# Layer 1's side products on a Trainium2 core: paired convolution taps, a bank sum on VectorE, and B with C in one step

## The chip, the cores and the metric

The kernel runs on one core of a Trainium2 chip. The metric is the device time of one launch in microseconds (us); lower is better. Engines are named as in the profile: PE is TensorE (matmul), PEld its weight loads, DVE is VectorE, ACT is ScalarE, POOL is GpSimd, and SP issues the DMAs. Everything is computed in fp32.

## The reference, cut to what matters

Four layers follow one another on x of shape (4, 64, 64, 64). Layers 0, 2 and 3 are not touched by the change. Layer 1 runs a state-space scan ("mamba") twice on each image, once along rows (w) and once along columns (h). For every one of 64 sequences of 64 tokens, with 192 channels and 96 states per channel:

```python
x1, res = jnp.split(x @ in_w.T, 2, axis=-1)
xc = causal depthwise convolution of x1 with K = 4 taps + conv_b      # cut
x1 = jax.nn.silu(xc)
A = -jnp.exp(jnp.clip(A_log, -5.0, 5.0))
x_dbl = x1 @ xproj_w.T
delta = jax.nn.softplus(x_dbl[..., :DTR] @ dproj_w.T + dproj_b)
B = x_dbl[..., DTR:DTR + N];  C = x_dbl[..., DTR + N:]
# selective_scan(u=x1): for each state n
c = jnp.exp(jnp.minimum(reversed cumulative sum of delta * A, 15.0))  # cut
x = jnp.cumsum(delta * u * B * c, axis=1) / (c + 1e-06)
y = jnp.einsum('bldn,bln->bld', x, C) + u * D
return y * jax.nn.silu(res) @ out_w.T
```

## The kernel before, in words

`layer1` calls `scan1` twice for each of the four images (d = 0 for w, d = 1 for h), so there are eight scans. A scan handles 4,096 tokens as 16 chunks of 256 tokens. A chunk has 2 tiles of 128 tokens; a tile's 128 partitions are two sequences of 64 tokens. Each tile goes through its 96 states in 12 blocks of 8 states, and each block in two units. A chunk is therefore 48 units, a scan 768 units, all scans 6,144 units. This text counts the units of a chunk from 0 to 47; units 0 and 24 open its tiles.

**The main work of a unit k** is the same everywhere:

- `expand(k+4)`: eight PE products write `z`; ACT makes two sigmoids of it, `e` and `r` (L1007). In every second unit POOL builds the two matrices `tB` and `dC` (L1015) and in the others SP copies a part of `r` across partitions by two DMAs (L1021).
- `weigh(k+1)` on DVE multiplies `e` by the token weights (L1030).
- `scan(k)` on PE computes the cumulative sums into the PSUM tile `S`, of which there is only one.
- `divide(k-1)` on DVE multiplies `S` into `r` (L1053). The next `scan` may not write `S` before that.
- `collect(k-1)` on PE adds the unit's share of y into the PSUM tile `y`, also a single one, of two banks. After the 24th unit of a tile ACT copies both banks into the SBUF tile `yt` (L1073).

**The side work** of a chunk is cut into steps: `pre` makes what the next chunk needs, `post` finishes a tile. A step is a small group of products on PE into the spare 128 columns of a `z` tile, an eviction on DVE one unit later, and sometimes elementwise work (`fs`) on DVE or ACT. `aside(k)` hands out one step per unit. The steps of `pre` are, in order: `conv` twice (8 products each), `res` twice, `dt` twice, `bc` four times (tile 0 and 1, B and C each), two steps of elementwise work alone, `after` twice, `utok` twice. `post` has `turn` (it transposes y and adds its two banks with it), a gate, and `out`. In a chunk they fall into units 1 to 18, and one more `turn` into unit 26. The gates multiply by a sigmoid (`res_gate`, and `yg` at L948); the four operations called `soft` (L885 to L888) make the softplus.

**The order** is written out by hand: `in_order` chains the instructions of PE, DVE, ACT and POOL, each engine on its own, in the order in which the loop issues them. In unit k DVE does `divide(k-1)`, then the eviction of the previous unit's step, then `weigh(k+1)`, then `fs`. PE does `scan(k)`, the `z` of k+4, `collect(k-1)`, then the step's products. ACT does the two sigmoids, then, where a tile has ended, the copy of y. SP is not chained. Chunk 0 of each scan has its side steps done one after another by `now`, before the loop.

Of the kernel before, what the change touches and what calls it, by code (L numbers as in the profile page):

```python
# [54 lines left out]
class Net:  # L55
# [229 lines left out]
    def setup_l1(self, sp, pp, d):  # L285
# [6 lines left out]
        P = slice(0, C) if d == "w" else slice(C, 2 * C)  # L292
        self.mm(ps[P, 0 : 2 * D1], hd, inw)
        w["wres"] = self.ctile([2 * C, D1], f"{n}_wres")[P]
        nc.vector.tensor_copy(w["wres"], ps[P, D1 : 2 * D1])
        cw = sp.tile([2 * C, 4, D1], F32, name=f"{n}_cw", tag="cw")[P]
        nc.sync.dma_start(cw, self.a[f"{n}_cw"].unsqueeze(0).to_broadcast([C, 4, D1]))
        w["wk"] = self.ctile([2 * C, 4, D1], f"{n}_wk")[P]
        for k in range(4):
            nc.vector.tensor_tensor(w["wk"][:, k, :], ps[P, 0:D1], cw[:, k, :], ALU.mult)  # L300
# [425 lines left out]
    def scan1(self, b, d, p, x1, x2):  # L726
# [30 lines left out]

        def pre(q, cx):
            n = f"b{b}{d}_{q}"
            T = lambda shape, tag, **k: p["q"].tile(shape, F32, name=f"{n}_{tag}", tag=tag, **k)  # L760
# [6 lines left out]
            dl = T([128, NTL, D1 + 16], "dl")  # L767
            d0 = s2 = dl[:, :, 0:D1]
# [8 lines left out]
            def conv(h):  # L777
                def mm(ps):
                    for i in range(2):
                        for k in range(4):  # L780
                            self.mm(
                                ps[0:DH, i, :], w["wk"][:, k, h * DH : (h + 1) * DH],
                                tokens(q, k)[:, 2 * i : 2 * i + 2], k == 0, k == 3,
                            )
# [8 lines left out]
            def res(h):  # L793
                def mm(ps):
                    for i in range(2):
                        self.mm(
                            ps[0:DH, i, :], w["wres"][:, h * DH : (h + 1) * DH],
                            tokens(q, 3)[:, 2 * i : 2 * i + 2],
                        )
# [19 lines left out]
            def bc(i, x):  # L819

                def mm(ps):
                    for s in range(2):
                        t0 = i * 128 + s * 64
                        for h in range(2):
                            self.mm(
                                ps[64 * s : 64 * s + 64, x, 0:N1], us[:, h, t0 : t0 + 64],
                                w["xbc"][:, h, x, s : s + N1].rearrange("p (i t) -> p t i", t=2),
                                h == 0, h == 1,
                            )

                def ev(ps):
                    nc.vector.tensor_copy(
                        BC[:, i, 2 * x : 2 * x + 2].rearrange("p t n -> p (t n)"), ps[:, x, 0:N1]
                    )
                    for s in range(2 * x):
# [6 lines left out]
            def utok(i):  # L842
# [6 lines left out]
                def ev(ps):  # L849
                    nc.vector.tensor_tensor(  # L850
                        half(wt[:, i]), half(dl[:, i, 0:D1]), ps[:, :, 0:DH], ALU.mult
                    )
# [3 lines left out]
            def after(i):  # L856

                def mm(ps):
                    for x in range(2):
                        for j in range(2):  # L860
                            c = (2 * x + j) * GC
                            self.mm(
                                ps[64 * j : 64 * j + 64, x, :], dl[:, i, c : c + 64], self.tri_after
                            )
# [12 lines left out]
            def first():  # L877
                nc.gpsimd.memset(dl[:, :, D1:], 0.0)
                nc.scalar.activation(u, dv, AF.Abs)
                nc.scalar.activation(u, u, AF.Sigmoid, bias=self.ln_half, scale=-1.0)  # L880
                nc.scalar.activation(s2, u, AF.Square)
# [3 lines left out]
                lambda: STT(po, po, ATANH[2], s2, ALU.add, ALU.mult),  # L885
                lambda: STT(po, po, ATANH[1], s2, ALU.add, ALU.mult),
                lambda: STT(po, po, ATANH[0], u, ALU.add, ALU.mult),
                lambda: STT(d0, dv, 0.0, po, ALU.max, ALU.add),  # L888
# [8 lines left out]
            step(bc(0, 0), first)  # L897
            step(bc(0, 1), res_gate[1])
            step(bc(1, 0), soft[0])
# [403 lines left out]
```

## Time and profile before

| what | us |
|---|---|
| median of 3 runs | 19620.61 |
| the runs | 19591.22 to 19622.32 |
| the profiled execution, its own time | 19619.08 |
| its span, first to last instruction | 19617.3 |
| the eight scans of layer 1 (sum of eight stretches of the trace) | 15222.6 |
| PE, DVE, ACT, POOL busy in the span | 17894.3, 16196.6, 12514.8, 8675.7 |
| mean granted PE clock | 0.965 |

The eight stretches are as long as the others within 1.1%, and in them the granted clock is 0.99 to 1.00. The change touches only these stretches (and a few instructions of the setup). A unit of the loop can be recognised in the trace by its `divide`, so the time from one `divide` to the next is the length of a unit. A matmul of the source is two matmul instructions in the trace, except a transpose, which is one.

### The profile page before, as it was taken

The numbers are of one execution on the slowest core, as the hardware profiler recorded it, in microseconds if no ns is written. First come the engines' busy times: TensorE is split into PE (matmuls) and PEld (weight loads), VectorE is DVE, ScalarE is ACT, GpSimd is POOL, SyncE is SP. The second block draws the span as 40 slices with busy tenths as digits, with TensorE's granted clock in tenths as the row PEclk, the third lists the DMA queues.
The fourth block names the chain that finished last, engine by engine and source line by source line (L and its number), as shares of the span: only waits on it lengthen the run. The fifth ranks groups of instructions, "written<-read, shape, count | busy, mean of one in ns | idle before, by whom it ended". The sixth has DMA issues, their size and how long they took to land. (4 is left out here: it accounts for less than half of the span.)

```text
span 19617.3 us, 623762 instructions
## 1 busy us (share of the span) xinstructions
PE 17894.3 (91%) x271560; PEld 11600.9 (59%) x271560; DVE 16196.6 (83%) x18938; ACT 12514.8 (64%) x15787; POOL 8675.7 (44%) x7068
## 2 busy tenths in 40 slices
PE   7999999997799999999779999999977999999996
PEld 2666666662266666666226666666622666666662
DVE  7788878887878887888788888888788888788878
ACT  4677767774467766776446776777644677677764
POOL 0455545551045554555115555555511555455551
PEclk9999999998999999999899999999988999999998
DMA  0233333330033333333003333333300333333320
GB/s 7 69 83 82 84 73 81 82 83 5 1 74 82 82 81 75 83 82 79 4 1 79 82 82 77 81 81 81 76 4 3 81 81 82 76 82 82 82 72 2
DMA packets 559944, 1265.03 MB, mean 64 GB/s; under 512 B 160568, under 2 KB 161824, under 8 KB 557216
## 3 DMA queue, kind: packets, MB, share of 16 engines
q1 hardware_dynamic: 557216, 1225.12, 26.0%
q8 instruction: 2144, 35.13, 0.8%
q14 instruction: 584, 4.78, 0.1%
HBM read 6.24 MB, written 4.19 MB: 1 GB/s over the span
## 5 line engine op out<-in xcount | busy, mean ns | idle before, releaser
L1007 ACT ACTIVATE b_k_e<-b_z,shift 128x768 f32<-128x768 f32 x6144 | 5533.4, 901 | 4501.7 <-PE b_z L120 3747.1
L1015 POOL TENSOR_TENSOR b_k_tB<-b_BC,tri 128x512 f32<-128x512 f32 x3072 | 3440.0, 1120 | 7456.0 <-PE b_u_S L120 6691.9
L1053 DVE TENSOR_TENSOR b_k_r<-b_u_S,b_k_r 128x768 f32<-128x768 f32 x6144 | 5858.1, 953 | 998.7 <-DMA b_k_r<-b_k_r 302.4
L1030 DVE TENSOR_TENSOR b_k_e<-b_k_e,b_wt 128x768 f32<-128x768 f32 x6144 | 6171.8, 1005 | 29.5 <-ACT b_k_e L1007 29.5
L120 PE MATMUL b_u_S<-b_k_e,b_k_tB 64*64 64x192 f32 x98304 | 5429.1, 335 | 598.5 <-DVE b_k_r L1053 507.2
L1007 ACT ACTIVATE b_k_r<-b_z,ln_eps 128x768 f32<-128x768 f32 x6144 | 5490.3, 894 | 0.0
L120 PE MATMUL b_y<-b_k_r,b_k_dC 64*64 64x192 f32 x98304 | 5194.2, 323 | 64.8 <-ACT b_yt L1073 62.4
L120 PE MATMUL b_z<-A,b_T 48*64 48x384 f32 x49152 | 5219.2, 487 | 4.5 <-ACT b_k_r L1007 4.3
L120 PEld LDWEIGHTS b_y<-b_k_r,b_k_dC 64*64 64x64 f32 x98304 | 3918.4, 133 | 2173.1 <-issue 1490.7
L1015 POOL TENSOR_TENSOR b_k_dC<-b_BC,ident 128x512 f32<-128x512 f32 x3072 | 4756.3, 1548 | 2.8 <-DMA b_BC<-b_BC 2.4
L120 PEld LDWEIGHTS b_u_S<-b_k_e,b_k_tB 64*64 64x64 f32 x98304 | 3280.0, 133 | 1867.4 <-DVE b_k_r L1053 1030.3
L120 PEld LDWEIGHTS b_z<-A,b_T 48*64 48x64 f32 x49152 | 1915.2, 135 | 225.3 <-DVE b_yg L922 57.8
L120 PE MATMUL d_y<-d_o,ident 128*128 128x512 f32 x1024 | 656.8, 775 | 416.5 <-DVE d_o L435 416.2
L432 POOL COPY l_state<-d_h 128x2 f32<-128x2 f32 x256 | 119.8, 468 | 1633.7 <-DVE d_h L429 1633.7
L120 PE MATMUL a_y<-a_o,ident 128*128 128x512 f32 x1024 | 575.9, 690 | 225.2 <-DVE a_o L435 223.3
L432 POOL COPY l_state<-a_h 128x2 f32<-128x2 f32 x256 | 110.5, 432 | 1418.9 <-DVE a_h L429 1418.9
L120 PEld LDWEIGHTS d_y<-d_o,ident 128*128 128x128 f32 x1024 | 213.6, 231 | 816.1 <-DVE d_o L435 620.3
L429 DVE TENSOR_TENSOR_SCAN a_h<-a_a,l_state,a_g 128x512 f32<-128x512 f32 x512 | 629.4, 1270 | 29.4 <-DVE a_g L418 0.5
L429 DVE TENSOR_TENSOR_SCAN d_h<-d_a,l_state,d_g 128x512 f32<-128x512 f32 x512 | 628.9, 1269 | 25.5
L407 ACT ACTIVATE d_a<-d_dl,l_A 128x512 f32<-128x512 f32 x512 | 339.2, 711 | 355.2 <-DVE d_dl L521 183.2
L407 ACT ACTIVATE a_a<-a_dl,l_A 128x512 f32<-128x512 f32 x512 | 336.1, 710 | 319.5 <-DVE a_h L429 160.9
L120 PEld LDWEIGHTS a_y<-a_o,ident 128*128 128x128 f32 x1024 | 189.9, 205 | 590.8 <-DVE a_o L435 377.3
(359 smaller groups left out, 11829.5 us busy)
## 6 DMA issues: line engine op xcount, KB each, us to landing
b_k_r<-b_k_r SPq DMA_DIRECT2D x6144, 192.0 KB, 2.9
b_BC<-b_BC SPq DMA_DIRECT2D x512, 12.0 KB, 1.8
xin<-in_x SPq DMA_DIRECT2D x16, 256.0 KB, 5.8
out<-d_so SPq DMA_DIRECT2D x32, 128.0 KB, 2.3
l1w_cw<-in_l1w_cw SPq DMA_DIRECT2D x1, 192.0 KB, 3.4
l1h_cw<-in_l1h_cw SPq DMA_DIRECT2D x1, 192.0 KB
t_l1w_in<-in_l1w_in SPq DMA_DIRECT2D x1, 144.0 KB, 2.2
t_l1w_xbc<-in_l1w_xbc SPq DMA_DIRECT2D x1, 144.0 KB
```

The source lines that it names most:

```text
L120: self.nc.tensor.matmul(out, lhsT=lhsT, rhs=rhs, start=start, stop=stop)
L407: nc.scalar.activation(a[:, t, :], dl, AF.Exp, scale=m["A"][:, j : j + 1])
L429: nc.vector.tensor_tensor_scan(h[:, t, :], now[:, t, :], g[:, t, :], st, ALU.mult, ALU.add)
L432: nc.gpsimd.tensor_copy(m["state"][:, 2 * i : 2 * i + 2], h[:, :, TOK - 1])
L1007: nc.scalar.activation(o.rearrange("p x (j c) -> p j x c", j=2), zin, AF.Sigmoid, bias=bias, scale=scale)
L1015: nc.gpsimd.tensor_tensor(out, m.unsqueeze(3).to_broadcast(shape), x.unsqueeze(1).unsqueeze(2).to_broadcast(shape), ALU.mult,)
L1030: nc.vector.tensor_tensor(e, e, chunks[q]["w"][:, i, :].unsqueeze(1).unsqueeze(2).to_broadcast([128, 2, 2, D1]), ALU.mult,)
L1053: nc.vector.tensor_tensor(r, S[k][:, :, 0:UC], r, ALU.mult)
```

## The change

1. **Two taps as one product.** Before, the convolution read the tokens from `x1` with 64 rows and 4 shifts: four products per output piece. Now `taps(q)` copies a chunk's tokens by two DMAs into a tile `xs` of 128 rows, the second half shifted by one token. The weights are laid out to match, and two products of 128 rows do the work of four of 64. `res` uses `xs` as well and takes the lower rows for one half and the upper rows for the other.
2. **Gates side by side.** `dl` gets a layout of four groups of 64 columns (48 used), so that `after` makes two products of 128 columns where it made four of 64. Elementwise operations on it read groups of 48.
3. **y's banks added and transposed.** ACT copies only the first bank of y to `yt`; a new DVE operation adds the second bank; `turn` then is two transposes in place of four accumulating products.
4. **B and C of a tile in one step.** `bc(i)` makes both for all 128 tokens, four products of 97 columns in place of eight of 96 that each covered 64 tokens; two DVE copies of 64 partitions each pick the even or odd order. The four `bc` steps become two, and the first two `soft` operations get steps of their own, as the last two had.

```diff
+        def taps(q):
+            xs = p["q"].tile([2 * C, QS, W + 3], F32, name=f"b{b}{d}_{q}_xs", tag="xs")
+            i, to = (3 + q * QS) * (W + 3), xs.rearrange("c h w -> c (h w)")
+            x = x1[d * C : (d + 1) * C].rearrange("c h w -> c (h w)")
+            size = QS * (W + 3)
+            nc.sync.dma_start(to[0:C], x[:, i : i + size])
+            nc.sync.dma_start(to[C:, 0 : size - 1], x[:, i + 1 : i + size])
+            return xs
...
         def pre(q, cx):
+            xs = cx["xs"]
+            if q + 1 < NQ:
+                chunks[q + 1]["xs"] = taps(q + 1)
...
-            dl = T([128, NTL, D1 + 16], "dl")
-            d0 = s2 = dl[:, :, 0:D1]
+            dl = T([128, NTL, 4, 64], "dl")
+            grouped = lambda x: x.rearrange("p i (g c) -> p (i g) c", c=GC)
+            d0 = s2 = dl.rearrange("p i g c -> p (i g) c")[:, :, 0:GC]
...
-                        for k in range(4):
+                        for k in range(2):
                             self.mm(
                                 ps[0:DH, i, :], w["wk"][:, k, h * DH : (h + 1) * DH],
-                                tokens(q, k)[:, 2 * i : 2 * i + 2], k == 0, k == 3,
+                                xs[:, 2 * i : 2 * i + 2, 2 * k : 2 * k + W], k == 0, k == 1,
                             )
...
-                    for s in range(2):
-                        t0 = i * 128 + s * 64
+                    for x in range(2):
                         for h in range(2):
                             self.mm(
-                                ps[64 * s : 64 * s + 64, x, 0:N1], us[:, h, t0 : t0 + 64],
-                                w["xbc"][:, h, x, s : s + N1].rearrange("p (i t) -> p t i", t=2),
-                                h == 0, h == 1,
+                                ps[:, x, 0 : N1 + 1], us[:, h, i * 128 : (i + 1) * 128],
+                                w["xbc"][:, h, x], h == 0, h == 1,
                             )
                 def ev(ps):
-                    nc.vector.tensor_copy(
-                        BC[:, i, 2 * x : 2 * x + 2].rearrange("p t n -> p (t n)"), ps[:, x, 0:N1]
-                    )
-                    for s in range(2 * x):
+                    for s in range(2):
+                        P = slice(64 * s, 64 * s + 64)
+                        nc.vector.tensor_copy(
+                            BC[P, i, 0:4].rearrange("p (x t) i -> p x t i", x=2),
+                            ps[P, :, s : s + N1].rearrange("p x (i t) -> p x t i", t=2),
+                        )
+                    for s in range(2):
                         nc.sync.dma_start(
...
-                        for j in range(2):
-                            c = (2 * x + j) * GC
-                            self.mm(
-                                ps[64 * j : 64 * j + 64, x, :], dl[:, i, c : c + 64], self.tri_after
-                            )
+                        self.mm(
+                            ps[:, x, :], dl[:, i, 2 * x : 2 * x + 2].rearrange("p g c -> p (g c)"),
+                            self.tri_after,
+                        )
...
-            step(bc(0, 0), first)
-            step(bc(0, 1), res_gate[1])
-            step(bc(1, 0), soft[0])
-            step(bc(1, 1), soft[1])
-            for f in soft[2:]:
+            step(bc(0), first)
+            step(bc(1), res_gate[1])
+            for f in soft:
                 step(None, f)
...
-                    for k in range(2):
-                        self.mm(
-                            ps[0:DH, h, :], yt[:, k, h * DH : (h + 1) * DH], self.ident, k == 0, k == 1
-                        )
+                    nc.tensor.transpose(ps[0:DH, h, :], yt[:, h * DH : (h + 1) * DH], self.ident)
...
-                yt = p["q"].tile([128, 2, D1], F32, name=f"{n}_yt", tag="yt", bufs=1)
-                nc.scalar.copy(yt, ys.pop(t)[:, :, 0:D1])
+                yt = p["q"].tile([128, D1], F32, name=f"{n}_yt", tag="yt", bufs=1)
+                y = ys.pop(t)
+                nc.scalar.copy(yt, y[:, 0, 0:D1])
+                sums.append(lambda: nc.vector.tensor_tensor(yt, y[:, 1, 0:D1], yt, ALU.add))
...
             if taken:
                 taken[0](taken[1])
                 taken = None
+            while sums:
+                sums.popleft()()
             S.pop(k - 1, None)
             scan(k)
```

## The prediction

> **What bounds the kernel now.** I read the page first, then the busy time of each engine in the eight stretches of layer 1, then single units in the timeline, since the shares are averages over two kinds of unit.
>
> ```profile
> PE 17894.3 (91%) x271560; PEld 11600.9 (59%) x271560; DVE 16196.6 (83%) x18938; ACT 12514.8 (64%) x15787; POOL 8675.7 (44%) x7068
> 5447.00:7350.00 1903.00, 1820.30 (x32572) 1307.69 (x32572) 1602.75 (x1926) 1342.06 (x1646) 1000.02 (x776) 1.00 0.34 82
> ```
>
> The second line is one scan: 1903 us, PE busy 1820, DVE 1603. PE looks like the bound, but its records overlap. The timeline at the start of the second tile of a chunk (unit 24 on) shows more:
>
> ```profile
> 5867.89 0.96 DVE L1053 TENSOR_TENSOR b_k_r<-b_u_S,b_k_r 128x768 f32<-128x768 f32 x1
> 5868.76 0.95 DVE L1030 TENSOR_TENSOR b_k_e<-b_k_e,b_wt 128x768 f32<-128x768 f32 x1
> 5869.85 0.96 DVE L1053 TENSOR_TENSOR b_k_r<-b_u_S,b_k_r 128x768 f32<-128x768 f32 x1
> 5870.12 0.48 ACT L1073 COPY b_yt<-b_y 128x384 f32<-128x384 f32 x1
> 5870.75 0.88 PE L120 MATMUL b_y<-b_k_r,b_k_dC 64*64 64x192 f32 x16 [0.32 <-ACT b_yt L1073]
> 5871.42 0.86 PE L120 MATMUL b_u_S<-b_k_e,b_k_tB 64*64 64x192 f32 x16
> 5872.39 0.96 DVE L1053 TENSOR_TENSOR b_k_r<-b_u_S,b_k_r 128x768 f32<-128x768 f32 x1 [0.58 <-PE b_u_S L120]
> 5873.51 1.11 PE L120 MATMUL b_z<-ident,b_yt 128*96 128x128 f32 x8
> 5874.66 0.60 DVE L922 SCALAR_TENSOR_TENSOR b_yg<-b_us,t_l1w_D,b_z 96x128 f32<-96x128 f32 x2 [1.31 <-PE b_z L120]
> 5876.05 0.95 DVE L1053 TENSOR_TENSOR b_k_r<-b_u_S,b_k_r 128x768 f32<-128x768 f32 x1
> ```
>
> A unit without side work lasts 1.96 us from divide to divide (5867.89 to 5869.85; 2.10 where POOL works beside it, 2.03 on average). DVE fills it (0.87 + 0.87 from start to start, so some 0.2 of rest), PE fills it too (0.69 + 0.66 + 0.68). And there is the loop scan, divide, scan through the single S: 0.88 + 0.96 plus about 0.1 of handover. All three ends are within 0.1 us. In a unit with side work PE adds the step's products at its end; DVE can evict them only then, and eviction, weigh and divide follow one another. So a side unit is bound by PE when its products are long, and by the chain "end of the products, eviction, weigh, fs, divide" when they are short or DVE has much to do. The start of a chunk:
>
> ```profile
> 5807.29 0.48 DVE L787 TENSOR_SCALAR b_v<-b_z,t_l1w_cb 96x256 f32<-96x256 f32 x1 [2.78 <-PE b_z L120]
> 5808.55 0.95 DVE L1053 TENSOR_TENSOR b_k_r<-b_u_S,b_k_r 128x768 f32<-128x768 f32 x1
> 5811.39 1.43 POOL L1015 TENSOR_TENSOR b_k_tB<-b_BC,tri 128x512 f32<-128x512 f32 x1 [5.68 <-PE b_u_S L120]
> 5811.83 1.53 DVE L948 TENSOR_TENSOR b_yg<-b_yg,b_us 96x512 f32<-96x512 f32 x1
> 5812.56 1.99 PE L120 MATMUL b_z<-x,l1w_wk 64*96 64x128 f32 x16
> ```
>
> DVE sat idle 2.78 us for the end of a conv: that unit is PE's. The gate at L948 took 1.53 us where the same shape takes 0.68 at L873, because POOL held something it needs.
>
> **The change, part by part.** Steps are priced from start to start of what follows, in the chunk that opens at 5801.59.
>
> *PE prices.* Conv is 16 instructions in 1.91 us (5812.56 to 5814.47), 0.120 each. The new conv is 8 instructions of 128 rows by 96 columns, 128 moving: the shape of turn, whose 8 took 1.04 (5873.51 to 5874.55, where the next scan starts), 0.130 each. [...] The row says 1.04; I take the row. New turn: two transposes; the nearest row is utok, also two transposes, 0.31 us for two at 96 columns; I take 0.34 (bounds 0.28 and 0.5). `after`: 4 full instructions for 8 half-wide ones that took 0.59; res, also 4, takes 0.61: no change. `res` may overlap its halves, 0.3 to 0.61, and does not matter: DVE with a gate ends its units. `bc` is where counting misleads:
>
> ```profile
> L120 PE MATMUL b_z<-l1w_xbc,b_us 96*64 96x96 f32 x1920 | 139.6, 263 | 0.0
> L120 PE MATMUL b_z<-l1w_wx,b_us 96*128 96x96 f32 x960 | 135.8, 285 | 0.0
> 5831.75 0.58 PE L120 MATMUL b_z<-l1w_xbc,b_us 96*64 96x96 f32 x8
> 5832.46 0.26 DVE L832 COPY b_BC<-b_z 128x96 f32<-128x96 f32 x1 [0.62 <-PE b_z L120]
> 5836.11 0.54 DVE L885 SCALAR_TENSOR_TENSOR b_dp<-b_dp,b_dl 128x384 f32<-128x384 f32 x1
> 5836.27 1.29 POOL L1015 TENSOR_TENSOR b_k_tB<-b_BC,tri 128x512 f32<-128x512 f32 x1 [3.40 <-PE b_u_S L120]
> ```
>
> The first two lines are groups (count, busy us), the others the timeline. The old products 64 columns wide go in pairs beside each other: 139.6 us for 1920 against 135.8 for 960 full-wide ones. The new step has wx's shape, 8 instructions, 1.07 us; two old steps took 2 x 0.51. So PE gains nothing, and what was spread over four units stands in two.
>
> *DVE prices.* The bank sum, 128x192 from PSUM and SBUF, is L850's shape: 0.35. The new copy on ACT is half as wide as 0.48; I take 0.30. A `bc` eviction is two copies of 192 elements: between 0.25 for 96 (L832) and 0.42 for 256 (L866), so 0.35, starting 0.26 apart. That the PSUM read has a step of two is in no row: 0.30 to 0.55, and I take 0.35.
>
> **Stage A, units 0 to 4** (t = 0 at 5801.59). Before: copy of y 2.24, first collect of the new tile 2.86, conv 3.67 to 5.66, divide(2) 6.96, divide(3) 11.70, divide(5) 17.4. After: DVE comes free at 0.87 but the sum waits for the copy, which ACT does behind both sigmoids: 2.54. Sum 2.62 to 2.97; weigh starts 2.89 in place of 0.87; divide(1) 3.8 in place of 1.96. The collect waits for the sum: 3.11; conv 3.87 to 4.98, hiding the late DVE; eviction 5.02, weigh 5.42, divide(2) 6.28. Turn 7.02 to 7.43 in place of 7.70 to 8.81; skip, weigh 7.99, and the gate behind POOL's tB as before, divide(3) 10.3. The second conv is then ready (10.6) before divide(3) ends (11.3), so only a part of its saving shows: divide(5) 15.85. Gain 1.55, of 2 x 0.87 + 0.70 = 2.44 that PE saves.
>
> **Stage C, units 24 to 27** (t = 0 at 5867.89), the same without a conv as cover. Sum 2.60 to 2.95; weigh 2.87; divide(25) 3.74 in place of 1.96; scan(26) can only start at 4.75 in place of 3.53: a loss of 1.2. Turn gives 0.70 back: divide(27) 8.68 in place of 8.16. Loss 0.5.
>
> **Stage B, units 9 to 12** (t = 0 at divide(9), 5830.89; before, divide(13) at 11.24). The first bc ends at 2.00 in place of 1.44; copies 2.06 and 2.32, weigh 2.58, gate 3.44, divide(10) 4.04 (before 3.32). Second bc 4.13 to 5.27; copies 5.33 and 5.59; weigh 5.85 to 6.8. Now POOL's tB, released by a scan that ends at 6.08, waits for weigh and is first in line; soft0 wants to start at 6.72 and stands behind it until 7.8. [...] The trace agrees twice (L948 1.53 against 0.68; L888 1.39 beside a POOL operation), but at soft0 before it shows 0.54, because tB came 0.16 after it (the lines above). [...] Then divide(12) 10.4 and divide(13) 12.6: loss 1.35. Before, soft0 and soft1 ran under bc products; now their units have only DVE work, 0.87 + 0.87 + 0.46 = 2.2.
>
> **Other parts.** The two taps DMAs of a chunk stand in SP's queue before the DMAs of r, 1.1 us of issue, and wait for nothing recent; an r has over 4 us from issue to use and lands in 2.9: nothing. If that cover were gone, every chunk would wait up to 1 us. POOL's memset is unchanged. In chunk 0 of a scan the slow conv (3.7 and 2.0 us there) is halved, bc and the sum give part back, and the first taps DMA lies beside the 5 us in which DVE builds A3: 0 to 4 us gain, I take 2. Sum: 128 x (-1.55 + 0.5 + 1.35) = +38, minus 8 x 2 = +22 us. The profiled execution took 19619 and the median is 19621, so this gives 19640.
>
> **The rivals.**
> 1. [...] If soft0 gets in front of tB in stage B, 0.9 us per chunk comes back at once, some 0.6 net of what runs behind: with the base loss gone, 128 x (-0.3) - 16 = -54; with cheaper evictions (0.30) as well another 0.2 per chunk: 19540 to 19565. For it: before, soft0 was first. Against: tB hangs on the scan's end, 0.5 us before soft0.
> 2. *Evictions with a step of two (slower).* Each 0.1 us on the four copies of a chunk lengthens the chain twice by 0.2 (the z products wait for these copies too): 128 x 0.4 = 51. At 0.55, a half rate, 19640 + 102 = 19742; with a longer sum 19770. It decides from 0.38 on, where the sum passes +0.2%. Against: L866 shows a PSUM copy at 1 ns an element.
> 3. *PE was the bound everywhere.* Then 2.44 + 0.70 per chunk are saved, 128 x 3.1 = 400, 19220. Against: the stall chain of stage C.
> 4. *Conv does not halve*, because 128-row products with alternating taps cost more than turn: at 0.24 each stage A loses its 1.5, 19830.
>
> **How the numbers follow.** A change of 0.2%, 39 us, is about what a measurement here tells from none. My base case, 19640 with 60 us either way, has 0.50: 0.05 faster, 0.25 within, 0.20 slower. Rival 1: 0.18, faster. Rival 2: 0.24, slower. Rival 3: 0.02, faster. Rival 4: 0.06, slower. So 0.25, 0.25, 0.50. The range reaches into rivals 1 and 2: 19530 to 19780.
>
> **What would show it.** Units 0 and 24 last 3.7 to 3.9 us, with DVE idle near 1.7 before the sum, released by ACT's copy; conv 8 instructions near 1.1; the first two bc units 3.2 and 4.1, with soft0 near 1.5; unit 11 and 12 near 2.2. The forecast is wrong if the sum does not wait, if soft0 stays at 0.54, or if the bc copies are not near 0.35.

## The result, and the profile after

The changed kernel took 19772.37 us (median of 4 runs, 19732.87 to 19777.21), the kernel before 19611.32 beside it: ratio 1.0079, 95% interval 1.0061 to 1.0096. Measured again later on another chip it was 19761.44, ratio 1.0071 (1.0059 to 1.0084). It is slower by 150 to 160 us; 19640 had been predicted.

The profiled execution took 19732.87 us (span 19731.2), 114 us more than that of before. First the page after: the busy times of the engines, and the group of the scan's products (busy us, mean ns, then idle us ahead of them and what ended most of it), with the same group before under it.

```profile
PE 17565.0 (89%) x264908; PEld 11269.3 (57%) x264908; DVE 16470.3 (83%) x19194; ACT 12492.4 (63%) x15787; POOL 8813.8 (45%) x7068
...
L120 PE MATMUL b_u_S<-b_k_e,b_k_tB 64*64 64x192 f32 x98304 | 5450.5, 336 | 970.4 <-DVE b_k_r L1070 696.3
...
L120 PE MATMUL b_u_S<-b_k_e,b_k_tB 64*64 64x192 f32 x98304 | 5429.1, 335 | 598.5 <-DVE b_k_r L1053 507.2
```

PE is busy 329 us less than before (17894.3), VectorE 274 us more (16196.6), and the scans now wait 970.4 us, most of it for `divide`; before it was 598.5. TensorE got less work and waits longer. The groups show which operations changed (the last line is soft0 before):

```profile
L909 DVE SCALAR_TENSOR_TENSOR b_dl<-b_dv,b_dp 128x384 f32<-128x384 f32 x128 | 177.9, 1390 | 0.3
L906 DVE SCALAR_TENSOR_TENSOR b_dp<-b_dp,b_dl 128x384 f32<-128x384 f32 x128 | 172.2, 1346 | 0.3
L850 DVE COPY b_BC<-b_z 64x192 f32<-64x192 f32 x480 | 170.6, 355 | 158.3 <-PE b_z L120 138.1
L120 PE MATMUL b_z<-l1w_xbc,b_us 96*128 96x97 f32 x960 | 135.9, 284 | 0.0
L120 PE MATMUL b_z<-b_xs,l1w_wk 128*96 128x128 f32 x960 | 134.0, 281 | 0.0
L1092 DVE TENSOR_TENSOR b_yt<-b_y,b_yt 128x192 f32<-128x192 f32 x256 | 91.5, 358 | 360.7 <-ACT b_yt L1091 360.3
...
L885 DVE SCALAR_TENSOR_TENSOR b_dp<-b_dp,b_dl 128x384 f32<-128x384 f32 x128 | 76.1, 594 | 0.0
```

The bank sum (L1092) waits 360 us for ACT's copy. The products for B and C of one direction take 135.9 us with 960 instructions, nearly as long as the 1920 of before (139.6 us). The first pass of the softplus (L906, soft0) takes 1346 ns where it took 594. A `bc` copy (L850) takes 355 ns, as assumed.

Lengths of units, from one `divide` to the next, in us (medians over chunks 1 to 14 of the eight scans; units not listed moved by less than 0.08):

| unit | 0 | 1 | 2 | 3 | 4 | 9 | 10 | 11 | 12 | 24 | 25 | 26 |
|---|---|---|---|---|---|---|---|---|---|---|---|---|
| before | 1.96 | 5.00 | 4.73 | 2.56 | 3.20 | 3.33 | 2.37 | 3.19 | 2.37 | 1.96 | 2.54 | 3.66 |
| after | 3.85 | 2.47 | 4.04 | 2.12 | 3.47 | 4.46 | 4.14 | 2.21 | 2.20 | 3.85 | 2.03 | 3.03 |

Stage A (units 0 to 4) went from 17.46 to 15.96, stage B (9 to 12) from 11.25 to 13.02, stage C (24 to 26) from 8.16 to 8.91. A chunk's mean went from 119.50 to 120.81.

Stage C in the timeline after (start, us, engine; t = 0 is `divide` at 5881.38):

```profile
5881.38 0.96 DVE L1070 TENSOR_TENSOR b_k_r<-b_u_S,b_k_r 128x768 f32<-128x768 f32 x1
...
5883.62 0.32 ACT L1091 COPY b_yt<-b_y 128x192 f32<-128x192 f32 x1
5883.97 0.36 DVE L1092 TENSOR_TENSOR b_yt<-b_y,b_yt 128x192 f32<-128x192 f32 x1 [1.63 <-ACT b_yt L1091]
...
5884.24 1.07 DVE L1047 TENSOR_TENSOR b_k_e<-b_k_e,b_wt 128x768 f32<-128x768 f32 x1
5884.45 1.76 POOL L1032 TENSOR_TENSOR b_k_dC<-b_BC,ident 128x512 f32<-128x512 f32 x1
5884.47 0.88 PE L120 MATMUL b_y<-b_k_r,b_k_dC 64*64 64x192 f32 x16 [0.55 <-DVE b_yt L1092]
...
5885.23 0.94 DVE L1070 TENSOR_TENSOR b_k_r<-b_u_S,b_k_r 128x768 f32<-128x768 f32 x1
```

VectorE idles 1.63 us ahead of the sum, the weigh is behind the sum, and `divide` comes at 3.85 in place of 1.96. Stage B in the timeline after (t = 0 at 813.93):

```profile
813.93 0.95 DVE L1070 TENSOR_TENSOR b_k_r<-b_u_S,b_k_r 128x768 f32<-128x768 f32 x1
...
814.79 1.13 PE L120 MATMUL b_z<-l1w_xbc,b_us 96*128 96x97 f32 x8
...
816.03 0.74 DVE L850 COPY b_BC<-b_z 64x192 f32<-64x192 f32 x2 [1.15 <-PE b_z L120]
...
816.80 0.96 DVE L1047 TENSOR_TENSOR b_k_e<-b_k_e,b_wt 128x768 f32<-128x768 f32 x1
...
817.68 0.68 DVE L894 TENSOR_TENSOR b_us<-b_v,b_us 96x512 f32<-96x512 f32 x1
...
818.39 0.96 DVE L1070 TENSOR_TENSOR b_k_r<-b_u_S,b_k_r 128x768 f32<-128x768 f32 x1
...
820.23 0.96 DVE L1047 TENSOR_TENSOR b_k_e<-b_k_e,b_wt 128x768 f32<-128x768 f32 x1
...
820.46 1.63 POOL L1032 TENSOR_TENSOR b_k_tB<-b_BC,tri 128x512 f32<-128x512 f32 x1 [4.55 <-PE b_u_S L120]
820.95 0.83 PE L120 MATMUL b_y<-b_k_r,b_k_dC 64*64 64x192 f32 x16
821.11 1.40 DVE L906 SCALAR_TENSOR_TENSOR b_dp<-b_dp,b_dl 128x384 f32<-128x384 f32 x1
...
823.64 0.88 PE L120 MATMUL b_u_S<-b_k_e,b_k_tB 64*64 64x192 f32 x16 [1.86 <-DVE b_k_r L1070]
```

The two copies of 0.355 span 0.74, so the second starts 0.38 behind the first, and the weigh starts 0.39 behind the second (816.03, 816.41, 816.80). soft0 starts behind POOL's tB and ends at 822.51, 0.42 after it. TensorE then has nothing to do for 1.86 us.

That gap had an effect which the prediction did not contain. Two chunks in one view of the windows (busy times of the engines, then the granted clock):

```profile
701.00:703.50 2.50, 0.91 (x20) 0.89 (x24) 2.47 (x4) 0.84 (x2) 1.36 (x2) 1.00 0.20 45
703.50:706.00 2.50, 2.50 (x48) 1.66 (x44) 2.50 (x5) 1.69 (x2) 0.24 (x1) 1.00 0.44 118
...
822.00:824.50 2.50, 0.86 (x20) 0.89 (x24) 2.47 (x4) 0.89 (x2) 1.41 (x2) 1.00 0.18 42
824.50:827.50 3.00, 3.00 (x41) 2.55 (x34) 2.53 (x4) 1.69 (x2) 0.00 (x0) 0.54 0.35 96
```

The same gap, and in the first chunk the clock stays at 1.00, in the second it falls to 0.54 behind it. In the trace it is at one half for 3.41 us each time. Such stretches begin in units 11 and 12 in 35 of the 120 chunks of the kernel after, in none of before. Unit 12 then lasts some 3.0 to 3.4 us in place of 2.20; its mean is 2.46. In 3 more chunks of the kernel after, such a stretch begins in unit 9.

### The profile page after: what moved, and what is told of

The parts are those of the page before. It is cut to its first block, busy times and chain, and to the rows that moved or that the text cites. A ratio compares the mean times of both kernels' runs of the same rounds, so it can differ in the third digit from the quotient of the medians.

```text
span 19731.2 us, 610401 instructions
## 1 busy us (share of the span) xinstructions
PE 17565.0 (89%) x264908; PEld 11269.3 (57%) x264908; DVE 16470.3 (83%) x19194; ACT 12492.4 (63%) x15787; POOL 8813.8 (45%) x7068
## 5 line engine op out<-in xcount | busy, mean ns | idle before, releaser
L120 PE MATMUL b_u_S<-b_k_e,b_k_tB 64*64 64x192 f32 x98304 | 5450.5, 336 | 970.4 <-DVE b_k_r L1070 696.3
L120 PEld LDWEIGHTS b_y<-b_k_r,b_k_dC 64*64 64x64 f32 x98304 | 3959.0, 133 | 2210.9 <-issue 1466.0
L1032 POOL TENSOR_TENSOR b_k_dC<-b_BC,ident 128x512 f32<-128x512 f32 x3072 | 4863.4, 1583 | 0.0
```

Of the source, the lines that this page charges most:

```text
L120: self.nc.tensor.matmul(out, lhsT=lhsT, rhs=rhs, start=start, stop=stop)
L1032: nc.gpsimd.tensor_tensor(out, m.unsqueeze(3).to_broadcast(shape), x.unsqueeze(1).unsqueeze(2).to_broadcast(shape), ALU.mult,)
```

## The experiments

All times are medians, each beside runs of the kernel before on the same chip (19611.5 to 19618.3 us).

**1. B and C back in four steps** (the rest as changed).

```diff
...
-            step(bc(0), first)
-            step(bc(1), res_gate[1])
-            for f in soft:
+            step(bc(0, 0), first)
+            step(bc(0, 1), res_gate[1])
+            step(bc(1, 0), soft[0])
+            step(bc(1, 1), soft[1])
+            for f in soft[2:]:
...
```

> The changed kernel with its fourth part alone undone: B and C of a tile again in two steps of four 64-column products each, with one contiguous copy per step, and the softplus's first two passes behind the last two of these steps; conv, turn and the side-by-side gates stay. My theory: what the one-step form costs is units 9 and 10 (4.46 and 4.14 us against 3.33 and 2.37), made of evictions in two pieces that end later and a softplus pass that is caught behind POOL's tB. Without it units 9 to 12 together go back from 13.0 to about 12.1 or less (the shorter dt and conv steps before them stay), some 0.7 us or more a chunk, so the time falls from 19772 to about 19500 and L906 goes back to some 0.6 us. The rival, that the sum of y's banks on VectorE is the loss: units 0 and 24 stay at 3.85 and carry it, units 9 to 12 hardly change, and the time stays at 19700 or above. A second rival, that TensorE's time counts (its xbc products are 271.8 ms-thousandths busy either way, so none is given back): no change within 40 us.

Measured: 19489.87 us, ratio 0.9933 (0.9918 to 0.9948). Units 9 to 12 are back at 11.24, all other units as after. So the fourth part turned a gain of 0.7% into a loss of 0.8%. The rivals fall: units 0 and 24 stayed at 3.85, and still the time fell by 272 us (from 19761).

**2. The bank sum taken back.** ScalarE copies both banks, four accumulating products turn them.

```diff
-                    nc.tensor.transpose(ps[0:DH, h, :], yt[:, h * DH : (h + 1) * DH], self.ident)
+                    for k in range(2):
+                        self.mm(
+                            ps[0:DH, h, :], yt[:, k, h * DH : (h + 1) * DH], self.ident, k == 0, k == 1
+                        )
...
-                nc.scalar.copy(yt, y[:, 0, 0:D1])
-                sums.append(lambda: nc.vector.tensor_tensor(yt, y[:, 1, 0:D1], yt, ALU.add))
+                nc.scalar.copy(yt, ys.pop(t)[:, :, 0:D1])
...
-            while sums:
-                sums.popleft()()
...
```

> The changed kernel with its third part alone undone: ScalarE copies both banks of y again, and the turn is again four products that accumulate, with no addition on VectorE. My theory: the addition waits on VectorE for a copy that stands behind two sigmoids, and the whole of units 0 and 24 (3.85 us against 1.96) is that wait, of which units 1 and 25 to 26 give back most, because the turn is then short and the weighs are early. Units 0, 24, 25 and 26 go back to about 2.0, 2.0, 2.5 and 3.7; unit 1 goes up again to about 4 to 5; stage A (units 0 to 4) is longer by about 1 us than in the changed kernel's 15.96, stage C shorter by 0.75, so the time lands at 19690 to 19800, near the changed kernel's. The rival, that the addition's wait is lost in full (1.9 us in each of two units of a chunk): the time falls by 2 x 1.9 x 128, less what the longer turn takes back, to about 19400.

Measured: 19719.35 us, ratio 1.005 (1.0035 to 1.0065), 42 under the changed kernel. Units 0, 24, 25 and 26 are 1.96, 1.96, 2.54 and 3.66; unit 1 is 4.13, unit 2 4.73. Stage A is 16.49, so with the sum it gains 0.53, about half of what was expected, and stage C loses 0.75. The wait of 1.9 us in each of two units is nearly all given back, as expected; what is left of part 3 is a small loss.

**3. The convolution alone** on the kernel of before.

```diff
...
-                        for k in range(4):
+                        for k in range(2):
                             self.mm(
                                 ps[0:DH, i, :], w["wk"][:, k, h * DH : (h + 1) * DH],
-                                tokens(q, k)[:, 2 * i : 2 * i + 2], k == 0, k == 3,
+                                xs[:, 2 * i : 2 * i + 2, 2 * k : 2 * k + W], k == 0, k == 1,
                             )
...
```

> The kernel of before with the first part of the change alone: two conv taps as one product over 96 partitions out of a copy of the images in which the second half is shifted by one column; the residual's products from the same copy; everything else as before. My theory: stage A shortens by what half of the conv's products take (1.91 to about 1.04 us a step, two steps, and units 1 to 4 are bound by these), about 1 us a chunk, and nothing after it moves: 19610 - 128 us - 20 us of shorter chunk starts = about 19460. The rival, that the saved product time is hidden because VectorE's evictions and the weighs bound these units: within 30 us of 19611.

Measured: 19441.98 us, ratio 0.9908 (0.9893 to 0.9922). Stage A is 16.49 in place of 17.46, and no other unit of chunks 1 to 14 moved. So of the 1.7 us of products that are saved in a chunk, 0.97 shows. The starts of the scans give more than the 20 us expected: chunk 0 is 4.7 us shorter in each of the eight scans, and the stretch from one scan of an image to the other is 4.7 us shorter in each of the four images.

**4. B and C in one step alone** on the kernel of before.

> The kernel of before with the fourth part of the change alone: B and C of a tile in one step of four 128-column products and two evictions of 64 partitions, the softplus's first two passes moved behind these steps. My theory: units 9 to 12 take 13 us or more against 11.24, as in the changed kernel (4.5, 4.1, 2.2, 2.2), and nothing pays for it: +1.7 us a chunk, about 19830. The rival, that in the changed kernel it is the other parts that delay units 9 and 10 (the turn or the gates): within 50 us of 19611. A second rival, that half the products help TensorE: faster than 19560.

Measured: 19846.05 us, ratio 1.0113 (1.0096 to 1.0129). Units 9 to 12 are 4.46, 4.14, 2.21 and 2.20, the numbers of the changed kernel. So it needs neither the turn nor the gates. The clock falls in units 11 and 12 in 49 of 120 chunks here. The four parts add up: in medians per chunk -0.97 (conv), +0.10 (gates side by side, which no run had alone; read from units 15 and 16), +0.22 (sum) and +1.77 (B and C) make +1.12, and the whole change has +1.14.

**5. A version meant to beat both.** Parts 1 and 3 only, with the weigh issued ahead of the sum:

```diff
...
+            early = bool(sums) and k + 1 < nu
+            if early:
+                weigh(k + 1)
             while sums:
                 sums.popleft()()
...
-            if k + 1 < nu:
+            if k + 1 < nu and not early:
                 weigh(k + 1)
```

> A version meant to beat both: conv's two taps as one product and the bank sum with the short turn, B and C and the gates' products as before, and in the unit in which the sum falls, VectorE issues the next weigh ahead of the sum, so that the wait for ScalarE's copy of y no longer holds the scan back. My theory: the scan of units 1 and 25 hangs on weigh and not on the sum; units 0 and 24 go from 3.85 to about 2.9, unit 1 to about 3.4, and the short turn pays in full. Stage A about 15.2, stage C near 9.8: together some 1.75 us a chunk under the kernel before, so 19618 - 1.75 x 128 - 20 = about 19370, under the 19442 of conv alone by 70. The rival, that what holds these units is the product stream of TensorE (collect waits for the sum, and scans stand behind collect), so that a weigh ahead of the sum brings nothing: 19410 to 19450, units 0 and 24 at 3.8.

Measured: 19347.9 us, ratio 0.9863 (0.9848 to 0.9877), the fastest of all. Units 0 and 24 are 2.86. Its timeline at the start of a second tile:

```profile
5788.24 0.96 DVE L1068 TENSOR_TENSOR b_k_r<-b_u_S,b_k_r 128x768 f32<-128x768 f32 x1
...
5789.11 0.95 DVE L1045 TENSOR_TENSOR b_k_e<-b_k_e,b_wt 128x768 f32<-128x768 f32 x1
...
5790.82 0.36 DVE L1090 TENSOR_TENSOR b_yt<-b_y,b_yt 128x192 f32<-128x192 f32 x1 [0.76 <-ACT b_yt L1089]
...
5791.10 0.95 DVE L1068 TENSOR_TENSOR b_k_r<-b_u_S,b_k_r 128x768 f32<-128x768 f32 x1
```

The sum still waits for ACT, but the weigh (0.95) lies in that wait. Against experiment 3 it is 94 us; in medians stage A is 0.46 shorter and stage C 0.24 (7.92 against 8.16).

**6. The copies without a step of two in PSUM.** It leaves out the sorting into even and odd positions.

```diff
-                            BC[P, i, 0:4].rearrange("p (x t) i -> p x t i", x=2),
-                            ps[P, :, s : s + N1].rearrange("p x (i t) -> p x t i", t=2),
+                            BC[P, i, 0:4].rearrange("p (x t) i -> p x (t i)", x=2),
+                            ps[P, :, s : s + N1],
```

> The changed kernel, but the two copies of a B-and-C step read PSUM contiguously and not with a step of two (the same sizes and the same 64 partitions; the sorting of even and odd positions is left out). What sets the 0.39 us from one copy to the next, where I had put 0.26? If it is the step of two: the copies take about 0.25 to 0.3 and start 0.26 to 0.3 apart, units 9 and 10 are shorter by 0.2 each, 19770 - 0.4 x 128 = about 19720. [...]

Measured: 19770.17 us, ratio 1.0077 (1.0062 to 1.0092); the mean of a copy is again 355 ns, and every unit is as long as after. The step of two costs nothing.

**7. One copy in place of two.** It leaves out the right order of the odd tokens' B and C.

```diff
-                    for s in range(2):
-                        P = slice(64 * s, 64 * s + 64)
-                        nc.vector.tensor_copy(
-                            BC[P, i, 0:4].rearrange("p (x t) i -> p x t i", x=2),
-                            ps[P, :, s : s + N1].rearrange("p x (i t) -> p x t i", t=2),
-                        )
+                    nc.vector.tensor_copy(
+                        BC[:, i, 0:4].rearrange("p (x t) i -> p x t i", x=2),
+                        ps[:, :, 0:N1].rearrange("p x (i t) -> p x t i", t=2),
+                    )
```

> The changed kernel with one copy over 128 partitions in place of the two over 64 in each B-and-C step (with the step of two in PSUM; the odd tokens' half then holds positions shifted by one, so their order is left out). My theory: the two copies of 64 partitions do not overlap, each costs 0.39 us from start to start, and VectorE's price does not depend on the partitions; so each of the steps loses 0.39, units 9 and 10 become about 4.07 and 3.75, soft0 stays behind tB at about 1.35, and the time is 19770 - 0.78 x 128 = about 19670. The rival, that the time of the unit is set by something else (z's products waiting, the gate): less than half of that, 19720 or more. A second rival, that an earlier weigh lets soft0 in front of tB: L906 at 0.6 and 19560.

Measured: 19593.15 us, ratio 0.9989 (0.9979 to 0.9998): 168 us under the changed kernel (19761), where about 100 was expected. Unit 9 is 3.84, so it loses 0.62 and not 0.39; unit 10 is 3.82. soft0 stays behind tB (1373 ns). Two things had been left out. The one copy of 0.36 is followed by the weigh 0.28 later, so it overlaps with it, where the changed kernel's copies of 64 partitions overlap with nothing (0.355 long, 0.38 and 0.39 from their start to that of the next), and the divide follows the gate after 0.60 in place of 0.71. And the clock falls in no unit 11 or 12 any more: TensorE's gap there is 1.48 us in place of 1.86. Its timeline:

```profile
820.57 0.36 DVE L848 COPY b_BC<-b_z 128x192 f32<-128x192 f32 x1 [1.15 <-PE b_z L120]
820.84 0.95 DVE L1045 TENSOR_TENSOR b_k_e<-b_k_e,b_wt 128x768 f32<-128x768 f32 x1
...
821.71 0.68 DVE L892 TENSOR_TENSOR b_us<-b_v,b_us 96x512 f32<-96x512 f32 x1
...
822.31 0.95 DVE L1068 TENSOR_TENSOR b_k_r<-b_u_S,b_k_r 128x768 f32<-128x768 f32 x1
...
827.23 0.88 PE L120 MATMUL b_u_S<-b_k_e,b_k_tB 64*64 64x192 f32 x16 [1.48 <-POOL b_k_dC L1030]
```

**8. An empty step ahead of soft0.**

```diff
             step(bc(1), res_gate[1])
+            step(None, lambda: None)
             for f in soft:
```

> The changed kernel with one empty step between the last B-and-C step and the first pass of the softplus, so that soft0 falls into the next unit, one without a PSUM eviction; everything behind it moves by one unit. It measures what the meeting of soft0 with POOL's tB costs. My theory: tB holds soft0 because the long eviction has put weigh and tB's release so close together; one unit later soft0 is issued ahead of tB, as in the kernel before, and L906 goes back from 1.346 to about 0.57. Unit 10 goes from 4.14 to about 2.9; but unit 11 takes soft0 (2.2 to 3.1), and one more unit carries a step, so that a chunk gets shorter by 0.3 to 0.5 us only: 19710 to 19740. The rival, that soft0 meets a tB in the next unit too: L906 stays over 1.2, unit 11 is near 3.5, and the time is 19770 or above. A second rival, that the meeting is the whole loss of the fourth part (1.77 us): 19560.

Measured: 19692.7 us, ratio 1.0035 (1.002 to 1.0049). soft0 is back at 547 ns, unit 10 at 2.83. But another operation takes long in its place:

```profile
831.32 1.04 POOL L1033 TENSOR_TENSOR b_k_dC<-b_BC,ident 128x512 f32<-128x512 f32 x1
831.36 1.81 DVE L1048 TENSOR_TENSOR b_k_e<-b_k_e,b_wt 128x768 f32<-128x768 f32 x1
```

Now a weigh takes 1.81 beside POOL's dC and unit 11 is 3.08; the third softplus pass (1387 ns) is caught in place of the last. Units 9 to 23 together are 38.92 us, and 38.90 after: in medians nothing is gained. What is left for the 69 us that the kernel gained against 19761 is the clock, which now falls in no unit 11 or 12 (experiment 9 shows what that is worth). So the time fell, a little further than the 19710 to 19740 expected and for another reason.

**9. TensorE's gap filled with products that nobody reads.**

```diff
-            for f in soft:
+            step((bc(1)[0], lambda ps: None), soft[0])
+            for f in soft[1:]:
                 step(None, f)
```

> The changed kernel with eight products more per chunk: the second B-and-C step's products are issued once more in the unit in which soft0 runs, and nothing reads them. They fall into TensorE's gap (821.78 to 823.64 in the changed kernel's profile), in which it waits for VectorE, and are over before the next scan can start. In the changed kernel's profile the granted clock falls to 0.5 for 3.41 us in units 11 and 12 in 35 of 120 chunks (in none before), and unit 12 then takes 3.0 to 3.4 us in place of 2.2: 0.26 us per chunk in the mean, some 31 us in all. My theory: it is TensorE's gap of 1.86 us that costs the clock there; with the gap cut to about 0.7 us no chunk loses it, unit 12 is 2.2 in all, and 960 instructions more make the kernel faster by about 30 us: 19740. The rival, that the dip belongs to this place for another reason (DMA traffic, VectorE at full load): the count of chunks with the dip stays at 30 or more and the time at 19770 or higher.

**10. The changed kernel again, on the same chip.**

> The changed kernel once more, as the base for the two beside it on the same chip: 19750 to 19790, and the dip of the clock in units 11 and 12 in 25 to 45 of 120 chunks.

Measured: 19698.82 us with the added products (ratio 1.0044, 1.0031 to 1.0056) and 19761.44 without (1.0071, 1.0059 to 1.0084). The clock falls in units 11 and 12 in 0 chunks with them and in 37 without. The medians of all units are equal; the mean of unit 12 is 2.19 against 2.47. The timeline with them:

```profile
832.74 0.83 PE L120 MATMUL b_y<-b_k_r,b_k_dC 64*64 64x192 f32 x16
832.90 1.40 DVE L906 SCALAR_TENSOR_TENSOR b_dp<-b_dp,b_dl 128x384 f32<-128x384 f32 x1
...
833.50 1.13 PE L120 MATMUL b_z<-l1w_xbc,b_us 96*128 96x97 f32 x8
...
835.43 0.88 PE L120 MATMUL b_u_S<-b_k_e,b_k_tB 64*64 64x192 f32 x16 [0.80 <-DVE b_k_r L1071]
```

The gap is 0.80, soft0 takes 1.40 as before, and more work makes the kernel 63 us faster (30 were expected; the spans of the two profiles differ by 40). So the gap is what costs the clock. Which chunks it hits can be seen in part: all changes of the clock lie on one grid of 3.413 us, to within 0.03 us over the whole run. In units 9 to 13 of the changed kernel there are 67 cells of that grid in which PE was busy for 0.52 of the time or less, and half the clock followed 38 of them; it followed none of the 482 fuller cells (cells that were at half the clock themselves are not counted). With the added products, and in experiments 7 and 11, no cell there is that empty. Why it did not follow the other 29 is open.

**11. The copies split by B and C** (two copies of 128 partitions and 96 elements; the right order of the odd tokens is left out).

```diff
-                    for s in range(2):
-                        P = slice(64 * s, 64 * s + 64)
+                    for x in range(2):
                         nc.vector.tensor_copy(
-                            BC[P, i, 0:4].rearrange("p (x t) i -> p x t i", x=2),
-                            ps[P, :, s : s + N1].rearrange("p x (i t) -> p x t i", t=2),
+                            BC[:, i, 2 * x : 2 * x + 2],
+                            ps[:, x, 0:N1].rearrange("p (i t) -> p t i", t=2),
                         )
```

> The changed kernel, but the two copies of a B-and-C step are split the other way: 128 partitions and 96 elements each in place of 64 partitions and 192 (the odd tokens' half then holds positions shifted by one, so their order is left out). It tells what of the price of the split is the number of instructions and what is the form. In the run with one copy the next instruction began 0.28 us after a copy of 0.36, so they overlapped; the two copies over 64 partitions began 0.39 apart and did not. Theory 1, a copy's time goes by its elements per partition and a follower starts before its end whatever the split: the copies take 0.25 and start some 0.25 or less apart, from first copy to weigh 0.45 to 0.5 in place of 0.78, units 9 and 10 are shorter by 0.3 to 0.4 each, and with the clock dip gone the time is about 19670. Theory 2, two copies in a row into one tile follow each other without overlap, with a fixed price of 0.39: no change, 19770.

Measured: 19601.66 us, ratio 0.9991 (0.9982 to 1.0001). The timeline:

```profile
5803.73 0.42 DVE L849 COPY b_BC<-b_z 128x96 f32<-128x96 f32 x2 [1.15 <-PE b_z L120]
5804.07 0.95 DVE L1046 TENSOR_TENSOR b_k_e<-b_k_e,b_wt 128x768 f32<-128x768 f32 x1
5804.94 0.68 DVE L893 TENSOR_TENSOR b_us<-b_v,b_us 96x512 f32<-96x512 f32 x1
5805.54 0.95 DVE L1069 TENSOR_TENSOR b_k_r<-b_u_S,b_k_r 128x768 f32<-128x768 f32 x1
```

From the first copy to the weigh it is 0.34 us (0.78 after; 0.45 to 0.5 expected), units 9 and 10 are 3.91 and 3.83, and there is no dip of the clock. Two instructions are not the price. What is left is the split over partitions, and it does two things at once: each copy has twice the elements per partition (192 in place of 96), and the two start at different partitions. The next experiment leaves the first alone and changes what follows from the second.

**12. The same two copies in the other order.**

```diff
-                    for s in range(2):
+                    for s in (1, 0):
                         P = slice(64 * s, 64 * s + 64)
```

> The changed kernel with the two copies of a B-and-C step in the other order: partitions 64 to 127 first, then 0 to 63. The same instructions, the same data. It asks why the two copies don't overlap. [...] Unit 9 goes from 4.46 to about 4.24, unit 10 from 4.14 to about 3.96: 0.40 us a chunk, 50 us in all, and perhaps some of the clock dips: 19761 becomes 19690 to 19715. The rival, that a copy of 64 partitions and 192 elements simply costs 0.39 before anything can follow: no change, 19750 to 19775, and the weigh still starts 0.39 behind the second copy.

Measured: 19669.5 us, ratio 1.0026 (1.0017 to 1.0035), 92 us under the changed kernel. The timeline:

```profile
817.96 0.72 DVE L850 COPY b_BC<-b_z 64x192 f32<-64x192 f32 x2 [1.15 <-PE b_z L120]
...
818.61 0.94 DVE L1047 TENSOR_TENSOR b_k_e<-b_k_e,b_wt 128x768 f32<-128x768 f32 x1
...
819.47 0.68 DVE L894 TENSOR_TENSOR b_us<-b_v,b_us 96x512 f32<-96x512 f32 x1
...
820.08 0.94 DVE L1070 TENSOR_TENSOR b_k_r<-b_u_S,b_k_r 128x768 f32<-128x768 f32 x1
...
822.32 2.03 POOL L1032 TENSOR_TENSOR b_k_tB<-b_BC,tri 128x512 f32<-128x512 f32 x1 [4.48 <-PE b_u_S L120]
...
822.90 0.54 DVE L906 SCALAR_TENSOR_TENSOR b_dp<-b_dp,b_dl 128x384 f32<-128x384 f32 x1
```

From the first copy to the weigh 0.65 (0.77 in the chunk shown above), the weigh 0.27 to 0.28 behind the second copy (0.39 in the change), and the divide 0.61 behind the gate (0.71): the rival, with the weigh still at 0.39, falls, since instructions and data are the same. Unit 9 is 4.22 (4.24 expected, an estimate of the author's). Unit 10 is 3.29 where 3.96 was expected, because soft0 now runs at once (0.54) and POOL's tB is the one that waits (2.03). The next pass is caught in its place (L907, 1365 ns mean), and unit 11 is 3.05. Units 9 to 12 together are 12.76, and no clock dip is left in units 11 and 12. The 0.26 us of stage B are some 31 us of the 92; the rest is of the size that the clock is worth in experiment 9.

## Why the prediction was right in its direction and too small

The time lies inside the range, the sign was the one given most chance, and the point was 130 us too low. Two things in this were luck. The time is only 8 us under the upper end of the range, and that end had been drawn for rival 2, whose cause experiment 6 refutes. And the base case had +22 us, less than the 39 that it called telling: what made the loss clear was the late starts behind the copies and the clock, neither of which it contained. Experiment 11, in which both are absent and the copies are shorter, does not differ clearly from before (ratio 0.9991, 0.9982 to 1.0001). Step by step:

- **PE prices.** From the start of a step's products to the start of the next scan: conv 1.05 us (5818.27 to 5819.32; 1.04 predicted from the old turn's row), turn 0.36 (5888.43 to 5888.79; 0.34), bc 1.06 (814.79 to 815.85; 1.07). Conv's weight loads took 164 and 158 ns with 64 rows in the two directions, 162 and 163 with 128, but the products don't go by their loads alone (0.131 us each where 16 of 64 rows took 1.91, 0.119 each), and the row priced them well. "PE gains nothing" for bc holds: 135.9 us against 139.6.
- **Stage A.** Right to within 0.11 us: divide(1) 3.85 (3.8), divide(2) 6.32 (6.28), divide(3) 10.36 (10.3), divide(5) 15.96 (15.85).
- **Stage C.** The mechanism is right, the size is not: a loss of 0.75 in place of 0.5. The mis-sized term is the weigh behind the sum: it was priced at 0.87 from start to start and took 0.99, with POOL's dC starting 0.21 after it and running beside it (its own length went from 0.95 to 1.07); the next scan followed at 4.94 in place of 4.75.
- **Stage B.** That soft0 would stand behind tB was right: it takes 1.40, and unit 12 is 2.20 as forecast. The loss of 1.35 in the sum is the author's estimate, and no run shows it: in the profile before soft0 took 0.54, with tB 0.16 behind it, and the changed kernel lost 1.77. The mis-sized term is "two copies of 192 elements ... 0.35, starting 0.26 apart". The durations were right; the second copy starts 0.38 behind the first, the weigh 0.39 behind the second, and the divide comes 0.11 later. The prediction says in its closing part that the first two units would be 3.2 and 4.1; its own working has 4.04 for the first, and 4.46 and 4.14 were measured.
- **Why 0.39.** Experiments 6, 11 and 12 rule out the PSUM step, the number of instructions and the form of 64 partitions by itself. Where the next start is not late, a copy of 0.36 is followed after 0.28 (experiment 7, and the last copy of experiment 12); a late start comes 0.01 to 0.03 after the end of the operation in front of it. Three starts are late in the changed kernel: the second copy (0.38 behind the first), the weigh behind it (0.39) and the divide (0.71 behind the gate, 0.60 in experiment 7). With the order of the copies turned round one of them stays: the second copy starts some 0.37 behind the first (two copies of 0.355 span 0.72), the weigh 0.27 to 0.28 and the divide 0.61 behind what is in front of them. So in these runs the weigh and the divide are late where the copy of partitions 64 to 127 was the last and not where that of 0 to 63 was; what makes them late no run shows. How much of stage B this is can be read in unit 9, where no operation of VectorE takes long beside POOL (weigh 0.96, gate 0.68). Experiment 11 has it 0.55 us shorter: 0.34 of this are the late starts (0.11 for the second copy, 0.12 for the weigh and 0.01 behind it, 0.11 for the divide), and 0.21 the halved elements per partition. In all of stage B the split over partitions costs 0.88 of the 1.77 (13.02 against 12.14). The other 0.89 was not taken apart; soft0 behind tB is in it (1339 ns in experiment 11, 594 before).
- **Not in the sum at all: the clock.** Half the clock for 3.41 us in 35 of 120 chunks; experiment 9 takes it away alone and gives 40 (spans of the profiled executions) to 63 us (medians). It is the one term that the sum lacked altogether.
- **Other parts.** "No change" for the gates side by side was off by 0.10 a chunk (units 15 and 16: 3.12 and 2.75, before 3.07 and 2.70). The taps DMAs cost nothing that can be seen, as said (2.2 and 2.1 us from issue to landing; in experiment 3, which has them, no unit of chunks 1 to 14 outside stage A moved). Chunk 0's steps run in the stretches between two scans: the four from one scan of an image to the other are 0.8 us shorter each (45.8 to 45.0), the three that also hold other layers 5.8 each (1022.9 to 1017.1), and what of the latter is chunk 0's is not shown. The 48 units of chunk 0 are shorter by 1 us in each scan. Together that is some 28 us, where 16 had been put.
- **The sum.** +0.30 us a chunk was predicted; +1.14 is measured in medians, +1.31 in the mean. Of the 0.84 between the first two, stage B is 0.42, stage C 0.25, the gates 0.10 and stage A 0.05. The sum also counts 128 chunks where the steps of `pre` run in 120, the last chunk of a scan having none; at 0.30 a chunk that is 2 us.
- **Rivals.** Rival 1 (soft0 in front of tB) did not happen in the change, but does in experiment 12, where its 0.9 us (an estimate of the author's; 1.40 against 0.54 is 0.86) are not gained, because another pass is caught. Rival 2 named a loss of this size, at these instructions, with a point of decision at 0.38; its cause, a slower read with a step of two, is refuted by experiment 6. Rival 3 (PE bound everywhere) asked for far more than any run gave: with all three other parts kept, experiment 1 is at 19490, not 19220. Rival 4 (conv does not halve) falls with experiment 3.

Open: in the change and in experiment 12 tB starts 0.23 and 0.28 after the weigh, both while it runs, and once POOL gets its turn ahead of soft0, once after it. In experiments 7 and 11 it starts 0.68 and 0.61 after the weigh and is ahead again. What decides was not found.

## What to carry to other kernels

Price a side step by what the engines behind it see, not by its instruction count: the same elements cost 0.88 us a chunk more when they were copied as two halves of the partitions and not as two halves of the columns, and turning the order of the two copies round won back 92 us without touching any work, about a third of it in the units themselves and the rest, by its size, with the clock. Issue what others wait for ahead of an operation that has to wait itself (the weigh ahead of the sum: units 0 and 24 of 2.86 in place of 3.85), and ask, when an engine gets less work, whether the new gap costs more than the work did. If parts of a change act in different stages, run them one by one: here one part was worth -0.9%, another +1.1%, and the sum hid both.

## What was not expected of the hardware

- A gap of 1.86 us in TensorE's work was enough for half the clock in 35 of 120 chunks; gaps of 1.48 us (experiment 7) and some 1.55 (experiment 11; an estimate: `collect` ends at 5808.91, `divide` starts at 5809.36, and 1.10 behind its start comes the scan, as in the change) were followed by it in none. In the trace of the profile after, the clock changes on a grid of 3.413 us: in units 9 to 13 half the clock followed 38 of the 67 cells in which PE was busy for 0.52 of the time or less, and none of the 482 fuller ones. Each of the 35 dips lasted 3.41 us, one cell.
- Eight products more in that gap made the kernel faster by 63 us, 40 in the spans of the two profiles.
- Taking apart a pair of operations of POOL and VectorE that take long beside each other (experiments 8 and 12) made another pair meet, at nearly the same price: soft0 takes 1.40 in place of 0.54 beside tB (the change), the pass after it 1.39 in place of 0.55 beside dC (825.10, experiment 12), a weigh 1.81 in place of 0.95 beside dC (experiment 8).
